# Query, key and value projections by one Strassen step in seven of eight images

## The chip, the cores and the metric

The kernel runs on one core of a Trainium2 chip. The metric is device time in microseconds (us) for one execution on the whole batch. TensorE (PE) multiplies matrices into PSUM; VectorE (DVE) and ScalarE (ACT) read PSUM and work on the on-chip memory SBUF; GpSimd (POOL) and SyncE (SP) mostly issue DMA transfers.

## What is computed

The batch has 8 images of 512 channels and 32 x 32 pixels, all in float32. Each image is group-normalised, goes through a block with two bottlenecks, and is added to its input. Cut to what matters:

```python
t = cbs(x, cv1_w, cv1_bn, 0)                    # 1x1 convolution, batch norm, silu
ys = [t[:, :C], t[:, C:]]                       # C = 256
for i in range(N):                              # N = 2 bottlenecks ("layers")
    yi = ys[-1]
    z = cbs(yi, m_cv1_w[i], m_cv1_bn[i], 1)     # 3x3 convolution
    z = bot_attention(z, m_qkv_w[i], m_rw[i], m_rh[i])
    z = silu(bn_eval(conv2d(z, m_cv2_w[i], 0), m_cv2_bn[i]))
    ys.append(yi + z)
return cbs(concatenate(ys, axis=1), cv2_w, cv2_bn, 0)

def bot_attention(x, qkv_w, rw, rh):            # 4 heads of 64
    q, k, v = conv2d(x, qkv_w, 0)               # 256 -> 3 x 256 channels, 1024 pixels
    logits = einsum('bhdi,bhdj->bhij', q, k + (rw + rh)) * 64 ** -0.5
    return einsum('bhij,bhdj->bhdi', softmax(logits), v)
```

So there are 16 projections to q, k and v: two layers in each of eight images. Each is a product of a 768 x 256 weight with a 256 x 1024 activation.

## The kernel before

Channels lie on the 128 partitions, so 256 channels are two blocks, called c, k or o in the code, and the 1024 pixels are two halves of 512. A loop over images, written out, runs per image: 3x3 convolution of layer 0 (`conv3x3`, matmuls at L756), projection (`project`), attention (`attention_fast`), 1x1 convolution `m2`, then the same for layer 1, then `cv2`. Parts of `cv1` of the next image, its group norm (`ahead` in layer 0), and parts of `cv2` are put behind attention groups by the dictionary `behind`. The convolutions use Winograd's scheme; `cv2` already uses a Strassen step (`strassen`) in all images but the last, with `product(..., onto=True)` accumulating a second product onto a PSUM tile that has been copied out in between.

`project` computes, for each c, kr (k plus the position terms rw and rh) and q: four matmuls of 512 columns each (two k blocks, two halves) into one PSUM tile (L321). ScalarE copies q out (L488); VectorE adds rw while it reads PSUM (L493), then rh (L494). v is computed transposed, with z as the stationary operand and 256 columns of weights moving (L505), and copied out by ScalarE (L510). In float32 each matmul appears in the trace as two records, each with its own weight load, so a projection has 32 records of 512 columns and 32 of 256.

`attention_fast` has four groups (c, half) of eight steps taken in pairs. A step computes logits into one PSUM tile (L540), ScalarE's exp writes them to a `pt` tile (L544), VectorE adds the pt tiles into `acc` for the softmax sums (L550, L552), and TensorE multiplies with v into `av` (L566), one pair behind the logits. At a group's end the sums go through a small matmul (L584), and `ao` is formed from `av` (L573, L574).

A tile framework orders the work: it gives each instruction a priority by its place in the program, plans each engine's order with a cost model when the program is built, and puts in the waits. `tc.issue_after` only adds an order on one engine. Tiles with the same tag share buffers: `big` in PSUM has three[...], `av` in PSUM one, `pt` three, and weights go through a ring `u` of five:

```python
def ring(shape, name):
    return const.tile(shape, F32, tag="u", name=name, bufs=5)
```

SP's DMA queue carries the loads into that ring, x, and the small transfers of the softmax sums; POOL's queue carries the residuals, the stores of the result and of prepared weights.

Of the kernel before, what the change touches and what calls it, by code (L numbers as in the profile page):

```python
# [52 lines left out]
P = 128  # L53
# [8 lines left out]
def kernel(  # L62
# [143 lines left out]
    def load_bottleneck(n):  # L206
        nc.sync.dma_start(qkv_sb[:, n], m_qkv_w[n].rearrange("(k p) o -> p k o", p=P))
        nc.sync.dma_start(rw_sb[:, n], m_rw[n].rearrange("(k p) f -> p k f", p=P))
        nc.sync.dma_start(rh_sb[:, n], m_rh[n].rearrange("(k p) f -> p k f", p=P))
        nc.sync.dma_start(m2_sb[:, n], m_cv2_w[n].rearrange("(k p) o -> p k o", p=P))  # L210

# [70 lines left out]
    def load_u(n, oc, i):  # L284
        u = new_u("u")
        nc.sync.dma_start(u, u_dram[n][oc][i])
        return u
# [7 lines left out]
    def img(ap):  # L295
        return ap.rearrange("p (h w) -> p h w", w=F)
# [4 lines left out]
    def stages(act, small, ps_big, ps_av, n_pt):  # L301
# [172 lines left out]
        def project(n, z):  # L474

            q = act.tile([P, NM, HW], F32, tag="q", name="q")
            kr = act.tile([P, NM, HW], F32, tag="k", name="kr")
            vT = act.tile([P, NJ, C], F32, tag="v", name="vT")

            def qk(c):  # L480
                for which in (1, 0):
                    o = which * C + c * P
                    ps = conv1x1(
                        lambda k: qkv_sb[:, n, k, o : o + P], lambda k, half: z[:, k, ts(half, HALF)], NM
                    )
                    for half in range(NH):
                        if which == 0:
                            nc.scalar.copy(q[:, c, ts(half, HALF)], ps[:, half, :])  # L488
                            continue
                        dst = img(kr[:, c, ts(half, HALF)])  # L490
                        rw = rw_sb[:, n, c, :].unsqueeze(1).to_broadcast([P, ROWS, F])
                        rh = rh_sb[:, n, c, ts(half, ROWS)].unsqueeze(2).to_broadcast([P, ROWS, F])
                        nc.vector.tensor_tensor(dst, img(ps[:, half, :]), rw, ALU.add)  # L493
                        nc.vector.tensor_tensor(dst, dst, rh, ALU.add)  # L494

            qk(0)
            per = NH * HALF // C
            for j0 in range(0, NJ, per):
                ps = ps_big.tile([P, per, C], F32, tag="big", name="v_ps")

                in_bank = per // NH
                for j in range(in_bank):
                    for k in range(NM):
                        for at in range(j, per, in_bank):
                            nc.tensor.matmul(  # L505
                                ps[:, at, :], z[:, k, ts(j0 + at, P)], qkv_sb[:, n, k, 2 * C : 3 * C],
                                start=(k == 0), stop=(k == NM - 1),
                            )
                for g in range(0, per, per // NH):
                    nc.scalar.copy(vT[:, j0 + g : j0 + g + per // NH, :], ps[:, g : g + per // NH, :])  # L510
            for c in range(1, NM):
                qk(c)
            return q, kr, vT

        def attention_fast(n, z, at, behind):

            q, kr, vT = project(n, z)
            behind.get(-1, lambda: None)()  # L520

            ao = act.tile([P, NM, HW], F32, tag="z", name="ao")
# [483 lines left out]
    for b in range(B):  # L1006
        more = b + 1 < B
        y1, y1n, y2 = ypad[b % 2], ypad[(b + 1) % 2], ypad[N]

        def u_of(n):  # L1010
            def of(oc):
                if b == 0 and oc == 1:
                    if n == 0:
                        with tc.issue_after(last.ins):
                            for i in range(PAIRS):
                                make(n, oc, [i])
                    else:
                        for k in range(NM):
                            raws[n, oc, k] = load_raw(n, oc, k, "kv"[k])
                        with tc.issue_after(last.ins):  # L1020
                            make(n, oc, [1])
                return [us.pop((oc, i)) if (oc, i) in us else load_u(n, oc, i) for i in range(PAIRS)]

            return of


        z = s.conv3x3(0, vs, u_of(0))
        if b == 0:
            load_bottleneck(1)
            raws[1, 0, 0] = load_raw(1, 0, 0, "y0", 2)  # L1030
            raws[1, 0, 1] = load_raw(1, 0, 1, "pt", 3)
        if more:
            xs = [load_x(act, b + 1, c, NX) for c in range(NX)]


        parts = {}


        norm = s.group_norm(xs) if more else iter(())
        groups = iter(range(NM * NH))  # L1040

        def ahead():
            nonlocal w1
            g = next(groups)
            next(norm, None)
            if g == 0:
                w1 = load_w1() if more else load_w2(1)
                if b > 0:
                    for at in ((0, 0), (0, 1), (0, 2), (1, 0)):
                        us[at] = load_u(1, *at)  # L1050
            if b == 0:
                if g == 0:
                    raws[1, 1, 0], raws[1, 1, 1] = load_raws_y0(1, 1)
                    make(1, 1, [2])
                    del us[1, 2]
                elif g <= NM:
                    make(1, 1, [0], [g - 1])

        def first():
            nonlocal nxt  # L1060
            if more:
                nxt = new_y0()
                s.cv1(w1, xs, nxt, y1n, Y1S[: NM // 2])
            else:
                parts[1] = s.cv2_part(w1, (y0, y1), 1)

        def second():
            if more:
                s.cv1(w1, xs, nxt, y1n, Y1S[NM // 2 :])
            else:  # L1070
                parts[2] = s.cv2_part(w1, (y0, y1), 2)

        NG = NM * NH
        behind = {g: ahead for g in range(NG)} | {NG: first, NG + 1: second}
        if b == 0:
            behind[-1] = lambda: make(1, 0, range(PAIRS))
        ao, check = s.attention_fast(0, z, b * N * NM * NH, behind)
        last = s.m2(0, ao, y1, lambda oc, half: inner(y2, oc, half))
        if more:
            s.cv1(w1, xs, nxt, y1n, Y0S)  # L1080
        else:
            parts[3] = s.cv2_part(w1, (y0, y1), 3)
            parts[0] = s.cv2_part(w1, (y0, y1), 0, range(NM))


        vs = s.tiles_in(y2)
        with tc.issue_after(last.ins):
            check()
        z = s.conv3x3(1, vs, u_of(1))
        w2 = ws = three = stored = None  # L1090
        begun = {}
        if b == 0:
            w2 = load_w2()

        def prepare():
            nonlocal stored, ws
            stored, ws = make_ws(w2)

        def ahead():
            nonlocal w2, three  # L1100
            if more:
                three = s.strassen(b, ws or load_ws(), y0, y1)
                for i in range(PAIRS):
                    us[0, i] = load_u(0, 0, i)
            else:
                w2 = load_w2()

        def first():
            if more:
                three[0]()  # L1110
            else:
                ks = range(NM, (1 + N) * NM)
                begun[0] = s.cv2_products(w2, (y0, y1, y2), 0, ks, ends=(ks[0], (2 + N) * NM - 1))

        def second():
            if more:
                three[1]()
            else:
                ks = range(2 * NM, (1 + N) * NM)
                begun[1] = ps_av.tile([P, NH, HALF], F32, tag="av", name="ps")  # L1120
                s.cv2_products(w2, (y0, y1, y2), 1, ks, begun[1], (ks[0], (2 + N) * NM - 1))

        behind = {1: ahead, NG: first, NG + 1: second}
        if b == 0:
            behind[0] = prepare
        ao, check = s.attention_fast(1, z, (b * N + 1) * NM * NH, behind)
        ylast = act.tile([P, NM, HW], F32, tag="v", name="ylast")
        last = s.m2(1, ao, y2, lambda oc, half: ylast[:, oc, ts(half, HALF)])
        with tc.issue_after(last.ins):
            check()  # L1130
        if more:
            three[2](y2, ylast, last, stored)
            with tc.issue_after(last.ins):
                vs = s.tiles_in(y1n)
        else:
            s.cv2(b, w2, (y0, y1, y2, ylast), begun, parts)
        y0 = nxt
# [94 lines left out]
```

## Time and profile before

| | |
|---|---|
| three timed runs | 2391.86 to 2392.54 us, median 2392.14 |
| span of the profiled execution | 2392.7 us |
| granted TensorE clock | 0.998 |
| L540 and L566, attention matmuls | 484.1 and 485.1 us, 4096 records each |
| L756, 3x3 convolutions | 307.9 us, 2720 records (and 40.8, 352) |
| L321 of the projections | 231.0 us, 512 records |
| L505, v of the projections | 115.8 us, 512 records |
| L544, exp | 494.9 us, 512 of 1023 ns |
| L552, softmax sums | 469.6 us, 384 of 1223 ns |
| L493 and L494, kr | 41.2 and 41.0 us, 64 of 686 and 682 ns |
| L488 and L510, copies of q and v | 34.4 us each, 64 of 589 ns |

A row is a group of instructions by line, engine and operation: busy time, count, mean duration. Matmuls are pipelined and their ends are modelled, so the mean duration of one is longer than the time until the next can start; starts in the timeline give the pitch. An engine's share of the span says little by itself; the waits say who waits for whom. A line such as `PE a L1 <- DVE b L2: 5.1, 5, 2.1` reads: TensorE, about to write a at line 1, waited for VectorE's b at line 2, 5.1 us in all, 5 times, the longest 2.1.

### The profile page before, as it was taken

To read this page: it belongs to the slowest core of one execution; us is meant where nothing else is said; L and a number is where in the kernel's file an instruction comes from. 1 tells how busy PE (TensorE), PEld (TensorE's weight loads), DVE (VectorE), ACT (ScalarE), POOL (GpSimd) and SP (SyncE) were. 2 spreads that over 40 slices of the span, in tenths; PEclk is the share of its full clock that TensorE was granted. 3 is DMA by queue.
4 is the path that set the end of the run, shared out by engine and by line. 5 is a ranking of instruction groups with operands and counts; after the bars stand their busy time and mean duration, and the time that the engine had idled before them with its cause. 6 is when DMAs were issued, how large, how long until landed. Compare 5 with 4: busy or idle time off the path is not lost.

```text
span 2392.7 us, 35333 instructions
## 1 busy us (share of the span) xinstructions
PE 2352.9 (98%) x14514; PEld 1176.4 (49%) x14514; DVE 1589.9 (66%) x2551; ACT 927.2 (39%) x1232; POOL 86.0 (4%) x301
## 2 busy tenths in 40 slices
PE   7999999999999999999999999999999999999998
PEld 4436355363553636446364453645536364463643
DVE  8866776666766667665586656766567765666654
ACT  1442524435244352433425344253432524326253
POOL 1000010000100001000010000100001000000001
PEclk9999999999999999999999999999999999999999
DMA  7412233030430305203161121601106020150202
GB/s 249 150 52 89 68 125 157 15 114 15 159 127 12 115 15 195 92 10 115 32 224 45 36 89 32 262 12 62 64 28 264 11 93 33 35 213 15 71 10 68
DMA packets 90728, 213.75 MB, mean 89 GB/s; under 512 B 27584, under 2 KB 49024, under 8 KB 77888
## 3 DMA queue, kind: packets, MB, share of 16 engines
q1 hardware_dynamic: 79360, 163.70, 20.0%
q0 software_dynamic: 11200, 47.72, 5.1%
q8 instruction: 116, 1.90, 0.3%
q14 instruction: 52, 0.43, 0.1%
HBM read 179.40 MB, written 31.98 MB: 88 GB/s over the span
## 4 chain that ended last, share of the span: by engine, by line
PE 93%; DVE 4%; DMA 1%; ACT 1%; issue 0%; SPq 0%; POOL 0%; DVEq 0%; ACTq 0%
PE ps L321 20%; PE av_ps L566 17%; PE l_ps L540 17%; PE c_ps L756 13%; PE c L811 8%; PE c_new L811 6%; PE m_ps L777 5%; PE v_ps L505 5%; DVE acc L552 1%; PE s_ps L584 1%; PE s_ps L602 1%; DMA rs<-r_dram 0%; DVE st L421 0%; DMA x<-in_x_dram 0%; DMA r_dram<-rc 0%
## 5 line engine op out<-in xcount | busy, mean ns | idle before, releaser
L544 ACT ACTIVATE pt<-l_ps 128x1024 f32<-128x1024 f32 x512 | 494.9, 1023 | 308.5 <-PE l_ps L540 307.0
L552 DVE TENSOR_TENSOR acc<-acc,pt 128x1024 f32<-128x1024 f32 x384 | 469.6, 1223 | 118.3 <-ACT pt L544 95.0
L566 PE MATMUL av_ps<-pt,vT 64*64 64x512 f32 x4096 | 485.1, 591 | 5.1 <-DVE ao L574 5.1
L540 PE MATMUL l_ps<-q,kr 64*64 64x512 f32 x4096 | 484.1, 590 | 0.0
L756 PEld LDWEIGHTS c_ps<-v_in,u 128*128 128x128 f32 x2720 | 306.7, 192 | 12.2 <-issue 9.7
L756 PE MATMUL c_ps<-v_in,u 128*128 128x128 f32 x2720 | 307.9, 275 | 4.6 <-DVE r_mid L388 1.7
L540 PEld LDWEIGHTS l_ps<-q,kr 64*64 64x64 f32 x4096 | 153.7, 133 | 278.6 <-issue 266.8
L566 PEld LDWEIGHTS av_ps<-pt,vT 64*64 64x64 f32 x4096 | 152.0, 133 | 281.5 <-issue 227.0
L321 PE MATMUL ps<-z,qkv_sb 128*128 128x512 f32 x512 | 231.0, 599 | 2.4 <-ACT z L306 2.1
L321 PE MATMUL ps<-x,w 128*128 128x512 f32 x512 | 227.5, 601 | 2.2 <-DVE x L455 2.2
L550 DVE TENSOR_TENSOR acc<-pt 128x1024 f32<-128x1024 f32 x64 | 78.4, 1225 | 134.0 <-ACT pt L544 134.0
L321 PEld LDWEIGHTS ps<-x,w 128*128 128x128 f32 x512 | 97.0, 192 | 130.6 <-issue 127.6
L493 DVE TENSOR_TENSOR kr<-ps,rw_sb 128x512 f32<-128x512 f32 x64 | 41.2, 686 | 178.1 <-PE ps L321 178.1
L321 PEld LDWEIGHTS ps<-z,qkv_sb 128*128 128x128 f32 x512 | 95.2, 191 | 110.4 <-issue 93.1
L811 PE MATMUL c_new<-t_in,ws 128*128 128x512 f32 x288 | 124.6, 592 | 0.0
L385 ACT COPY m<-c_ps 128x256 f32<-128x256 f32 x96 | 35.5, 370 | 227.7 <-PE c_ps L756 219.5
L505 PE MATMUL v_ps<-qkv_sb,z 128*128 128x256 f32 x512 | 115.8, 379 | 0.6 <-DVE r_ends L389 0.6
L777 PE MATMUL m_ps<-ao,m_sb 128*128 128x512 f32 x256 | 112.5, 592 | 0.0
L505 PEld LDWEIGHTS v_ps<-qkv_sb,z 128*128 128x128 f32 x512 | 97.2, 190 | 27.8 <-issue 16.2
L811 PEld LDWEIGHTS c_new<-t_in,ws 128*128 128x128 f32 x288 | 54.7, 190 | 68.9 <-issue 66.0
L306 ACT ACTIVATE m_kept<-m_kept,bh,sh 128x512 f32<-128x512 f32 x42 | 31.9, 806 | 146.0 <-DVE m_kept L895 86.3
L640 DVE TENSOR_TENSOR ao<-ao,rs 128x512 f32<-128x512 f32 x64 | 44.1, 688 | 63.4 <-DMA rs<-r_dram 62.8
(170 smaller groups left out, 2144.8 us busy)
## 6 DMA issues: line engine op xcount, KB each, us to landing
u<-u SPq DMA_DIRECT2D x85, 1024.0 KB
x<-in_x_dram SPq DMA_DIRECT2D x32, 512.0 KB
x_res<-in_x_dram POOLq DMA_DIRECT2D x28, 512.0 KB, 8.9
out_dram<-m_kept POOLq DMA_DIRECT2D x28, 512.0 KB, 7.5
w<-in_cv_w_dram SPq DMA_DIRECT2D x13, 1024.0 KB
u<-u_new POOLq DMA_DIRECT2D x12, 1024.0 KB, 5.8
rs<-r_dram SPq DMA_DIRECT2D x96, 128.0 KB
ws<-s SPq DMA_DIRECT2D x24, 512.0 KB
```

Source lines behind the costliest of these rows:

```text
L321: nc.tensor.matmul(ps[:, half, :], w_of(k), rhs_of(k, half), start=(k == begin), stop=(k == end))
L493: nc.vector.tensor_tensor(dst, img(ps[:, half, :]), rw, ALU.add)
L505: nc.tensor.matmul(ps[:, at, :], z[:, k, ts(j0 + at, P)], qkv_sb[:, n, k, 2 * C : 3 * C], start=(k == 0), stop=(k == NM - 1),)
L540: nc.tensor.matmul(ps[kh * HD : (kh + 1) * HD, hd, :], kr[r, c, o : o + HD], q[r, c, ts(half, HALF)], start=True, stop=True,)
L544: exp = nc.scalar.activation(pt[:, i], ps, AF.Exp, scale=SCALE)
L550: return nc.vector.tensor_tensor(accs[g], pt[:, 0], pt[:, 1], ALU.add)
L552: ins = nc.vector.tensor_tensor(accs[g], accs[g], pt[:, i], ALU.add)
L566: nc.tensor.matmul(avs[g][hd * HD : (hd + 1) * HD, kh, :], vT[r, j, o : o + HD], pt[r, i, hd, :], start=(j == 0), stop=(j == NJ - 1),)
L640: nc.vector.tensor_tensor(dst, dst, rs, ALU.mult)
L756: nc.tensor.matmul(ps[:, row, col, :], us[i][:, k, row, SLOT[col], :], vs[i][:, k, row, col, :], start=(k == 0), stop=(k == NM - 1),)
L777: nc.tensor.matmul(pss[oc][:, half, :], m2_sb[:, n, k, ts(oc, P)], ao[:, k, ts(half, HALF)], start=(k == 0), stop=(k == NM - 1),)
L811: nc.tensor.matmul(ps[:, o, :], w[:, k, ts(o, P)], rhs[part][:, c, :], start=(k == 0 and not onto), stop=(k == KB - 1), skip_group_check=onto,
```

## The change

A layer's weights are split in 2 x 2 blocks A (output block o, input block i; each block holds the 128 columns of q, k and v), z in 2 x 2 blocks B (channel block, pixel half). Four sums s1 to s4 of weight blocks are made once per layer, in the second attention of image 0, written to DRAM, and loaded into the ring with the convolution's second output block in images 1 to 7. Four sums t1 to t4 of z's blocks are made in each projection. Seven products replace eight; two pairs of them accumulate in PSUM (`onto=True`), with the first of each copied out (u, m5) in between. q, kr and v then come from sums on VectorE. Tiles t, u and m5 take the three `pt` buffers. Image 0 keeps `project`.

```diff
+    def make_sq(n):
+        (a11, a12), (a21, a22) = ([block_qkv(n, o, i) for i in range(2)] for o in range(2))
+        parts = [act.tile([P, 2, 3, P], F32, tag="x", name="sq_new", bufs=NX) for _ in range(2)]
...
+        nc.vector.tensor_tensor(s1, a21, a22, ALU.add)
+        nc.vector.tensor_tensor(s2, s1, a11, ALU.subtract)
+        nc.vector.tensor_tensor(s3, a11, a21, ALU.subtract)
+        nc.vector.tensor_tensor(s4, a12, s2, ALU.subtract)
+        for h, t in enumerate(parts):
+            nc.gpsimd.dma_start(sq_dram[n][:, 2 * h : 2 * h + 2], t)
+
+    def load_sq(n):
+        w = ring([P, 4, 3, P], "sq")
+        nc.sync.dma_start(w, sq_dram[n])
+        return w
...
+        def project_strassen(n, z, sq):
...
+            def product(ps, v, w, rhs, onto=False):
+                for o in range(2):
+                    nc.tensor.matmul(
+                        ps[:, o, :], w[:, o, :], rhs, start=not onto, stop=True, skip_group_check=onto
+                    )
+                for j in range(HALF // P):
+                    nc.tensor.matmul(
+                        v[:, ts(j, P)], rhs[:, ts(j, P)], w[:, 2, :], start=j == 0 and not onto, stop=True,
+                        skip_group_check=True,
+                    )
...
+            tt(t1, b12, b11, ALU.subtract)
+            ps_a, ps_b, ps_v = big(), big(), ps_av.tile([P, 2, HALF], F32, tag="av", name="pv_ps")
+            u, m5 = kept("u_z"), kept("m5_z")
+            product(ps_a, ps_v[:, 0], block_qkv(n, 0, 0), b11)
+            nc.scalar.copy(u[:, 0:2], ps_a)
+            nc.scalar.copy(u[:, 2], ps_v[:, 0])
+            product(ps_b, ps_v[:, 1], s1, t1)
+            nc.scalar.copy(m5[:, 0:2], ps_b)
+            nc.scalar.copy(m5[:, 2], ps_v[:, 1])
+            tt(t2, b22, t1, ALU.subtract)
+            tt(t3, b22, b12, ALU.subtract)
+            tt(t4, t2, b21, ALU.subtract)
+            product(ps_a, ps_v[:, 0], block_qkv(n, 0, 1), b21, onto=True)
+            q0, _, v0 = places(0, 0)
+            nc.scalar.copy(q0, ps_a[:, 0])
+            add_r(0, 0, ps_a[:, 1])
+            nc.scalar.copy(v0, v_of(ps_v[:, 0]))
+            product(ps_b, ps_v[:, 1], s4, b22, onto=True)
+            q1, k1, v1 = places(0, 1)
+            nc.scalar.copy(k1, ps_b[:, 1])
+            nc.scalar.copy(q1, ps_b[:, 0])
+            nc.scalar.copy(v1, v_of(ps_v[:, 1]))
+            ps_c, ps_w = big(), big()
+            product(ps_c, ps_w[:, 0], s2, t2)
+            tt(u[:, 0:2], ps_c, u[:, 0:2], ALU.add)
+            tt(u[:, 2], ps_w[:, 0], u[:, 2], ALU.add)
+            tt(k1, k1, u[:, 1], ALU.add)
+            add_r(0, 1)
+            tt(v1, v1, v_of(u[:, 2]), ALU.add)
+            tt(q1, q1, u[:, 0], ALU.add)
+            ps_d = big()
+            product(ps_d, ps_w[:, 1], s3, t3)
+            q2, k2, v2 = places(1, 0)
+            q3, k3, v3 = places(1, 1)
+            tt(k2, ps_d[:, 1], u[:, 1], ALU.add)
+            tt(q2, ps_d[:, 0], u[:, 0], ALU.add)
+            tt(v2, v_of(ps_w[:, 1]), v_of(u[:, 2]), ALU.add)
+            ps_e, ps_v = big(), ps_av.tile([P, 2, HALF], F32, tag="av", name="pv_ps")
+            product(ps_e, ps_v[:, 0], block_qkv(n, 1, 1), t4)
+            tt(k3, k2, m5[:, 1], ALU.add)
+            tt(q3, q2, m5[:, 0], ALU.add)
+            tt(v3, v2, v_of(m5[:, 2]), ALU.add)
+            tt(v2, v2, v_of(ps_v[:, 0]), ALU.subtract)
+            tt(k2, k2, ps_e[:, 1], ALU.subtract)
+            tt(q2, q2, ps_e[:, 0], ALU.subtract)
+            for half in range(NH):
+                add_r(1, half)
+            return q, kr, vT
...
-            q, kr, vT = project(n, z)
+            q, kr, vT = project(n, z) if sq is None else project_strassen(n, z, sq)
...
-                return [us.pop((oc, i)) if (oc, i) in us else load_u(n, oc, i) for i in range(PAIRS)]
+                got = [us.pop((oc, i)) if (oc, i) in us else load_u(n, oc, i) for i in range(PAIRS)]
+                if b > 0 and oc == 1:
+                    sq[n] = load_sq(n)
+                return got
...
-            behind[0] = prepare
+            behind |= {0: prepare, 2: lambda: make_sq(0), 3: lambda: make_sq(1)}
```

`add_r(c, half)` adds rw and then rh to kr in two operations; `places` names the parts of q, kr and v for an output block and a half.

## The prediction

> **What bounds the kernel now.** First I read the page: busy time of each engine, and the chain of work that ended last.
>
> ```profile
> PE 2352.9 (98%) x14514; PEld 1176.4 (49%) x14514; DVE 1589.9 (66%) x2551; ACT 927.2 (39%) x1232; POOL 86.0 (4%) x301
> ...
> PE 93%; DVE 4%; DMA 1%; ACT 1%; issue 0%; SPq 0%; POOL 0%; DVEq 0%; ACTq 0%
> ```
>
> TensorE is busy in all but 40 us, and the chain runs through it for 93%. Next the waits of TensorE, longest first:
>
> ```profile
> PE gm_ps L427 <- DVE mv L422: 11.6, 1, 11.6
> PE av_ps L566 <- DVE ao L574: 5.1, 5, 2.1
> PE ps L321 <- DVE x L455: 2.2, 1, 2.2
> PE ps L321 <- ACT z L306: 2.1, 2, 1.2
> ```
>
> The first is the start of the program; what is left is small. So a microsecond of matmul saved is a microsecond saved, provided that no new wait takes its place. Then the stage itself, a projection in a middle image, as the timeline of TensorE shows it (start, duration, records; consecutive groups overlap in their modelled ends, so I take differences of starts):
>
> ```profile
> 960.69 3.60 PE L321 MATMUL ps<-z,qkv_sb 128*128 128x512 f32 x8
> 964.13 1.03 PE L505 MATMUL v_ps<-qkv_sb,z 128*128 128x256 f32 x4
> 965.18 3.70 PE L321 MATMUL ps<-z,qkv_sb 128*128 128x512 f32 x8
> 968.72 6.21 PE L505 MATMUL v_ps<-qkv_sb,z 128*128 128x256 f32 x28
> 974.76 7.03 PE L321 MATMUL ps<-z,qkv_sb 128*128 128x512 f32 x16
> 981.72 3.66 PE L540 MATMUL l_ps<-q,kr 64*64 64x512 f32 x32
> 985.21 1.90 PE L566 MATMUL av_ps<-pt,vT 64*64 64x512 f32 x16
> ```
>
> From first projection matmul to first logit 981.72 - 960.69 = 21.03 us, with no gap; the second layer has 1118.08 - 1097.05, the same. VectorE in that stretch:
>
> ```profile
> 963.86 0.42 DVE L414 SCALAR_TENSOR_TENSOR z<-sd,r_ends 128x256 f32<-128x256 f32 x1
> 967.20 1.29 DVE L493 TENSOR_TENSOR kr<-ps,rw_sb 128x512 f32<-128x512 f32 x2 [2.92 <-PE ps L321]
> 968.41 1.28 DVE L494 TENSOR_TENSOR kr<-kr,rh_sb 128x512 f32<-128x512 f32 x2
> 978.39 1.29 DVE L493 TENSOR_TENSOR kr<-ps,rw_sb 128x512 f32<-128x512 f32 x2 [8.70 <-PE ps L321]
> 979.60 1.28 DVE L494 TENSOR_TENSOR kr<-kr,rh_sb 128x512 f32<-128x512 f32 x2
> 984.85 1.22 DVE L550 TENSOR_TENSOR acc<-pt 128x1024 f32<-128x1024 f32 x1 [3.96 <-ACT pt L544]
> 986.18 2.56 DVE L552 TENSOR_TENSOR acc<-acc,pt 128x1024 f32<-128x1024 f32 x2
> 988.65 1.87 DVE L421 BATCH_NORM_STATS2 st<-x 128x6 f32<-128x512 f32 x3
> ```
>
> It is mostly idle here. A 512-wide operation follows its neighbour after 0.605 us (968.41 - 967.20 for two). ScalarE:
>
> ```profile
> 964.32 1.52 ACT L306 ACTIVATE z<-z,bh,sh 128x512 f32<-128x512 f32 x2 [3.00 <-DVE z L414]
> 965.85 1.28 ACT L310 ACT_TABLE_LOAD   x1
> ```
>
> The second channel block of z ends at 965.84, 5.15 us after the convolution's last matmul was issued; today the k=0 matmuls and four v records fill that.
>
> **What the Trainium skill says.** "VectorE: DVE Perf Modes", section on the TRN2 errata, prices a float32 tensor_tensor at (N+151)/0.96 ns: 691 and 1224 ns for 512 and 1024; the trace has 686 (L493) and 1223 (L552). "TensorE: Matmul & The Clock Gate", section "Back-to-back issue gap", says that spacing is set by the matmul and its weight load together. The trace agrees: 192 convolution records of 128 columns took 21.44 us (1075.61 to 1097.05), 0.1117 each, against 0.1072 for a quarter of the 512-column pitch of 0.429. "ScalarE: Activation LUTs", section "What ACT_TABLE_LOAD costs", gives 1283 ns for a load; the trace shows 1283.
>
> **The change, part by part**, for the 14 projections of images 1 to 7.
>
> *TensorE.* Removed: 32 records of 512 columns and 32 of 256, 21.03 us. Added: seven products of 4 records of 512 and 8 of 128. 28 x 0.429 = 12.01; 56 x 0.1117 = 6.26; for 14 switches of shape 0.03 each, from the 0.1 and 0.04 us by which the 512-to-256 switches above exceed their pitch, 0.4. Sum 18.7. Gross gain 2.3 us a projection; bounds 2.0 (0.05 a switch, records of 0.115) and 2.75 (no switch cost).
>
> *VectorE.* 18 new operations, 17 of 512 and one of 1024: 17 x 0.605 + 1.13 = 11.4 us of pitch on top of the eight kr additions. *ScalarE:* eight copies of 0.589 become seven and two of 1.01, 1.4 us more, hidden in its gaps. What matters is order. Write T for the end of issue of the fifth product (s2, t2). TensorE then has two products, 2 x 2.67 = 5.3 us, and wants the first logit. VectorE has, from T - 0.7: u (1.13) and u of v, k1, two r additions, v1, q1, then k2, q2, v2 (done T + 6.05; q2 at T + 5.4), k3, q3, v3 (T + 7.85), the three subtractions (T + 9.65), four r additions (T + 12.1). The logits need PSUM: three big tiles, which the products hold. The first comes free with q2, some 0.2 us late; the next with v2; the third only at T + 9.65, so the third logit tile reuses the first after its exp. A tile takes 0.86 to fill (half of 1.72 for 16 records) and about 0.2 + 0.94 (3.77 / 4) to be drained, so four tiles on two buffers take about 4.0 us instead of the trace's 3.49: 0.2 + 0.5, and 0.1 for handing over. So 0.8, within 0.3 and 1.1.
>
> *The start of the projection.* The first two products need only z's first block and last 5.3 us, just over the 5.15. But the third and fourth accumulate onto PSUM that ScalarE must have copied, and the copies of m5 queue behind the silu and the table load: 965.84 + 1.5 + 1.01 + 0.59 = 968.9, where the fourth product wants them at 968.6 to 970. Bounds 0 and 1.35 (if the third product's v matmuls wait for m5's v copy, which lies in the same PSUM tile); I take 0.2.
>
> *After the projection.* VectorE is free for the softmax sums about 6.6 us after the first logit, not 3.1. Queued behind are the adds that free the three pt tiles, the first group's sums (before: last add 996.51, wanted 999.05) and the addition that frees the single av tile. In layer 1 gaps of 0.35, 0.88 and 1.79 us absorb it. In layer 0 four batch statistics of 0.6 us follow at once, slack is 2.5 us, and about 1 us can reach TensorE unless matmuls are reordered. Bounds 0 and 2; mean over layers 0.2.
>
> *DMA, ring, image 0.* A load of 768 KB joins SP's queue with the second half of the convolution's weights; its slot comes free a third of the way through the convolution, 14 us ahead of use, and a 1 MB transfer on the POOL queue lands in 5.8 us. Queued behind are x loads, w1 and later weights, wanted tens of us later, so nothing. Two stores on POOL lie beside attention. Eight 384-wide operations (0.55 us: 4.4 us) in image 0's second attention are fitted into VectorE's gaps of 0.8 to 1.8 us; 0 to 4, I take 1.
>
> *Sum.* 14 x (2.3 - 0.8 - 0.2 - 0.2) = 15.4; less 1 is 14.4. Against its own span, 2392.7 - 14.4 = 2378.3. The three timed runs have 2391.86 to 2392.54, so 2378.
>
> **The rivals.** *Nothing waits:* the order found fills every gap (as it does now around the silu) and the gross gain stays, 14 x 2.3 = 32 us, 2360. For: TensorE's waits are near zero today. Against: PSUM is full at the seam. *VectorE sets the seam (slower):* the place is from the fifth product to the end of the first attention group. It decides from 2.3 us of waiting a projection. If each of the 18 new operations costs 0.1 us more in semaphores or dependent issue (dependent neighbours show 0.72, not 0.605), the chain is 1.8 later: logits 0.8 + 1.2, layer 0's group end 1 + 1.9 averaged over two layers 1.45, sum 3.45 with none at the start; a loss of 1.15 x 14 = 16 us, 2408. For: VectorE at the seam has no slack on paper. Against: two thirds of it is idle elsewhere, and the adds can be interleaved. *Break-even:* ScalarE's m5 copies cost their full 1.35 and the seam 0.8, 2.15 against 2.3: 2390. *The change does not do what it says:* the products also need shape-switch time above 0.16 us, taking the whole gain; the trace's attention alternates shapes of weights every 16 records at 0.107 without loss, so unlikely.
>
> **How the numbers follow.** Forecast 0.44; nothing waits 0.26; break-even 0.12; slower seam 0.16; matmuls no faster 0.02. Break-even is shared between same and slower or faster: faster than 0.2% (4.8 us, about what a measurement of this kernel can tell from no change) 0.44 + 0.26 + 0.02 of it = 0.72; same 0.09; slower 0.19. The range reaches to 2359 for the full gain and to 2404 into the slower case; the forecast's own range is 2368 to 2386.
>
> **What would show it.** Right: 28 and 56 records a projection, 18.6 to 18.8 us of TensorE, first logit 18.9 to 19.6 us after the first product, a wait of the logits for VectorE (q2 or v2) of a few tenths, VectorE busy near 1770 us. Wrong: TensorE waiting over 1 us for m5's copy or for the av tile; 128-column records at 0.13 or more; VectorE's chain ending later than 13 us after the fifth product; weight loads of a product waiting for the sq load.

## The result, and the profile after

The changed kernel took 2383.66 us (median of 6 runs, 2381.73 to 2385.39), the kernel before 2391.92 beside it: ratio 0.9966, with a 95% interval from 0.9954 to 0.9979. That is 8.3 us, or 0.34%, where 14 us were forecast. The profiled execution has a span of 2383.3 us, 9.4 under before's 2392.7.

The page of the changed kernel, busy time of the engines and the chain:

```profile
PE 2326.4 (98%) x14794; PEld 1168.9 (49%) x14794; DVE 1751.7 (73%) x2811; ACT 947.7 (40%) x1246; POOL 88.1 (4%) x305
...
PE 81%; DVE 13%; DMA 4%; issue 2%; ACT 1%; SPq 0%; POOL 0%; DVEq 0%; ACTq 0%
```

TensorE has 26.5 us less to do, VectorE 162 more. VectorE's part in the chain rises from 4 to 13%, that of DMA from 1 to 4%: more of the program now ends behind them. TensorE's longest waits (the wait at the program's start, 10.8 us, is left out) name the place:

```profile
PE l_ps L656 <- DVE q L626: 12.2, 14, 0.9
...
PE av_ps L682 <- DVE ao L690: 6.5, 11, 2.1
PE l_ps L656 <- ACT pt L660: 4.0, 14, 0.3
PE c_ps L872 <- DMA u<-u: 2.8, 4, 1.5
```

Three waits are new. The two of the logits (`l_ps`) come 14 times each, once a projection; the one for loads into the ring comes in four convolutions and is taken up at the end. The timeline of TensorE at the same projection as before shows the first two in square brackets. Its lines are the first product's q and k, the v matmuls of the sixth, the last product, the four logit tiles and the first av matmul:

```profile
956.92 1.88 PE L556 MATMUL p_ps<-z,qkv_sb 128*128 128x512 f32 x4
...
971.77 1.05 PE L560 MATMUL p_ps<-sq,t_z 128*128 128x128 f32 x8
972.66 1.88 PE L556 MATMUL p_ps<-t_z,qkv_sb 128*128 128x512 f32 x4
974.38 1.05 PE L560 MATMUL pv_ps<-qkv_sb,t_z 128*128 128x128 f32 x8
975.45 1.95 PE L656 MATMUL l_ps<-q,kr 64*64 64x512 f32 x16
977.68 1.09 PE L656 MATMUL l_ps<-q,kr 64*64 64x512 f32 x8 [0.29 <-ACT pt L660]
979.64 1.09 PE L656 MATMUL l_ps<-q,kr 64*64 64x512 f32 x8 [0.87 <-DVE q L626]
980.55 1.90 PE L682 MATMUL av_ps<-pt,vT 64*64 64x512 f32 x16
```

From first product to first logit is 975.45 - 956.92 = 18.53 us, where it was 21.03: 2.5 won. From first logit to first av matmul is 5.10, where it was 3.49: 1.61 lost. The brackets count idle time after the modelled end of a matmul, so differences of starts are the better measure. VectorE in that stretch: the read that drains the fifth product (takes it out of PSUM), two reads of the sixth, the last read of the seventh, and the first softmax sum:

```profile
969.36 1.23 DVE L606 TENSOR_TENSOR u_z<-p_ps,u_z 128x1024 f32<-128x1024 f32 x1 [2.46 <-PE p_ps L556]
...
974.71 0.68 DVE L617 TENSOR_TENSOR q<-p_ps,u_z 128x512 f32<-128x512 f32 x1
975.31 0.68 DVE L618 TENSOR_TENSOR vT<-p_ps,u_z 128x512 f32<-128x512 f32 x1
...
978.90 0.68 DVE L626 TENSOR_TENSOR q<-q,p_ps 128x512 f32<-128x512 f32 x1
...
981.91 1.22 DVE L666 TENSOR_TENSOR acc<-pt 128x1024 f32<-128x1024 f32 x1
```

L626 ends at 979.58, and the fourth logit tile starts 0.06 later: it takes the buffer of the seventh product. In the table, made of differences of starts in one traced execution of each kernel, "projection" is first product to first logit, "seam" first logit to first av matmul, and "rest" first av matmul to the start of `m2`, in layer 0 and in layer 1. The value is that of most images, or about the median where they scatter. The times in us are medians of several runs, the ratios are to the kernel before on the same chip.

| kernel | projection | seam | rest, layer 0 / 1 | us | ratio (95%) |
|---|---|---|---|---|---|
| before | 21.03 | 3.49 | 69.8 / 68.85 | 2391.92 | |
| after | 18.52 | 5.10 | 70.2 / 68.85 | 2383.66 | 0.9966 (0.9954 to 0.9979) |
| no_sums | 18.44 | 3.49 | 69.8 / 68.85 | 2358.87 | 0.9859 (0.9844 to 0.9874) |
| three_before | 19.80 | 5.10 | 70.2 / 68.85 | 2400.91 | 1.0040 (1.0025 to 1.0056) |
| three_after | 19.80 | 5.10 | 70.2 / 68.86 | 2401.73 | 1.0043 (1.0028 to 1.0059) |
| chain_before | 19.73 | 4.34 | 71.56 / 68.85 | 2398.18 | 1.0028 (1.0017 to 1.0038) |
| chain_after | 18.52 | 5.10 | 71.53 / 68.85 | 2391.51 | 1.0004 (0.9995 to 1.0012) |
| drain7 | 18.52 | 3.60 | 71.71 / 68.9 | 2371.72 | 0.9923 (0.9910 to 0.9937) |
| drain7_pool4 | 18.52 | 3.60 | 72.2 / 68.9 | 2376.50 | 0.9938 (0.9925 to 0.9952) |
| drain7_pool8 | 18.52 | 3.48 | 71.13 / 69.48 | 2371.34 | 0.9914 (0.9899 to 0.9930) |
| drain7_r_later | 18.52 | 3.60 | 71.5 / 68.9 | 2374.59 | 0.9927 (0.9913 to 0.9940) |
| drain7_stats | 18.52 | 3.60 | 74.8 / 68.9 | 2390.95 | 0.9997 (0.9989 to 1.0006) |
| before_stats | 21.03 | 3.49 | 74.76 / 68.86 | 2418.28 | 1.0105 (1.0090 to 1.0121) |
| drain7_r_early | 18.45 | 3.48 | 69.8 / 68.85 | 2358.36 | 0.9862 (0.9846 to 0.9879) |

### The profile page after: what moved, and what is told of

Same layout as the page of the kernel before. It is cut to its first block, busy times and chain, and to the rows that moved or that the text cites. A ratio compares the mean times of both kernels' runs of the same rounds, so it can differ in the third digit from the quotient of the medians.

```text
span 2383.3 us, 36285 instructions
## 1 busy us (share of the span) xinstructions
PE 2326.4 (98%) x14794; PEld 1168.9 (49%) x14794; DVE 1751.7 (73%) x2811; ACT 947.7 (40%) x1246; POOL 88.1 (4%) x305
## 4 chain that ended last, share of the span: by engine, by line
PE 81%; DVE 13%; DMA 4%; issue 2%; ACT 1%; SPq 0%; POOL 0%; DVEq 0%; ACTq 0%
PE av_ps L682 16%; PE l_ps L656 14%; PE ps L344 12%; PE c_ps L872 11%; PE c L927 8%; PE c_new L927 6%; PE p_ps L556 5%; PE m_ps L893 5%; DVE acc L668 3%; PE pv_ps L560 2%; DMA u<-u 2%; DVE st L444 1%; PE s_ps L700 1%; DVE acc L666 1%; DVE u_z L606 1%
## 5 line engine op out<-in xcount | busy, mean ns | idle before, releaser
L656 PE MATMUL l_ps<-q,kr 64*64 64x512 f32 x4096 | 491.2, 593 | 16.3 <-DVE q L626 12.2
L927 PEld LDWEIGHTS c_new<-t_in,ws 128*128 128x128 f32 x288 | 54.7, 190 | 68.9 <-issue 66.0
L329 ACT ACTIVATE t<-m_ps,bh,sh 128x512 f32<-128x512 f32 x64 | 48.1, 776 | 83.9 <-PE m_ps L893 82.5
L556 PE MATMUL p_ps<-t_z,sq 128*128 128x512 f32 x168 | 81.3, 593 | 0.0
L373 POOL MEMSET w_rows<- 128x16 f32 x96 | 12.3, 128 | 1831.9 <-PE s_ps L700 1137.8
L893 PEld LDWEIGHTS m_ps<-ao,m_sb 128*128 128x128 f32 x256 | 48.6, 190 | 61.2 <-issue 61.2
L329 ACT ACTIVATE z<-z,bh,sh 128x512 f32<-128x512 f32 x64 | 48.6, 806 | 50.9 <-DVE z L437 50.8
```

The costliest lines, as they stand in the source:

```text
L329: return nc.scalar.activation(dst, src, AF.Silu, scale=sh[:, k : k + 1], bias=bh[:, k : k + 1])
L556: nc.tensor.matmul(ps[:, o, :], w[:, o, :], rhs, start=not onto, stop=True, skip_group_check=onto)
L656: nc.tensor.matmul(ps[kh * HD : (kh + 1) * HD, hd, :], kr[r, c, o : o + HD], q[r, c, ts(half, HALF)], start=True, stop=True,)
L893: nc.tensor.matmul(pss[oc][:, half, :], m2_sb[:, n, k, ts(oc, P)], ao[:, k, ts(half, HALF)], start=(k == 0), stop=(k == NM - 1),)
L927: nc.tensor.matmul(ps[:, o, :], w[:, k, ts(o, P)], rhs[part][:, c, :], start=(k == 0 and not onto), stop=(k == KB - 1), skip_group_check=onto,
```

## The experiments

The theory: the products save at least what was forecast, and VectorE's chain of sums gives most of it back, at first by holding PSUM. The rival: VectorE's backlog as such, the late softmax sums, costs the time. A second rival: something else in the change does, such as loads or copies.

**no_sums**: everything behind the fifth product on VectorE left out.

```diff
-            tt(u[:, 0:2], ps_c, u[:, 0:2], ALU.add)
...
-            tt(k2, ps_d[:, 1], u[:, 1], ALU.add)
...
+            nc.scalar.copy(k2, ps_d[:, 1])
+            nc.scalar.copy(q2, ps_d[:, 0])
+            nc.scalar.copy(v2, v_of(ps_w[:, 1]))
...
+            nc.scalar.copy(k3, ps_e[:, 1])
```

> All seven products stay, but the sums on VectorE behind the fifth product are left out: the fifth product is not read, and q, k and v of the second block are plain copies of products six and seven by ScalarE (so q, k and v are not the reference's). It bounds what the products alone bring. Theory: projection 18.5 us, seam 3.5 us, group ends as before: the kernel is 14 x (2.51 + 0.0) = 35 us under before, with the 2.5 us of other differences 2353 to 2358. Rival (something else in the change costs the time, such as the loads of the weight sums, the larger SP queue or the copies on ScalarE): 2365 or more.

It took 2358.87, 33 us under before, just above the 2353 to 2358 expected and clear of the second rival's 2365. Projection and seam are as expected; 14 x 2.59 = 36 us is their worth from the starts. So the seven products with their loads, copies and z's sums are worth about 33 us, and the sums behind them cost 25. The second rival falls.

**drain7**: ScalarE, idle at that time, copies the seventh product out.

```diff
+            e7 = act.tile([P, 2, HALF], F32, tag="acc", name="e_z", bufs=2)
+            nc.scalar.copy(e7, ps_e)
...
-            tt(k2, k2, ps_e[:, 1], ALU.subtract)
-            tt(q2, q2, ps_e[:, 0], ALU.subtract)
+            tt(k2, k2, e7[:, 1], ALU.subtract)
+            tt(q2, q2, e7[:, 0], ALU.subtract)
```

> The seventh product's PSUM tile is copied to SBUF by ScalarE, which is idle there, instead of being held until VectorE has subtracted it. Theory (PSUM tiles held by VectorE's chain set the seam): the third big tile comes free about 1 us after the last product instead of 4 us, the time from first logit to first av matmul falls from 5.10 to 3.5 to 3.8 us, and 14 x 1.3 to 1.6 = 18 to 22 us are won against the changed kernel: 2362 to 2366 us, ratio to before about 0.988 to 0.990. Rival (VectorE's backlog as such, the late softmax sums and the v sums behind them, sets the seam): VectorE has as much to do as before, so at most 0.3 us a projection, 2379 to 2384.

The seam fell to 3.60 as the theory has it; 14 x 1.5 = 21 us. But the kernel won only 12 and landed between the two forecasts. TensorE's timeline in a layer 0 projection (first logits, first av; then the sums of the first group and the next av tile) shows where the rest went, and one line of VectorE, the first softmax sum, shows why:

```profile
970.85 3.66 PE L658 MATMUL l_ps<-q,kr 64*64 64x512 f32 x32
974.45 1.95 PE L684 MATMUL av_ps<-pt,vT 64*64 64x512 f32 x16
...
989.12 0.64 PE L702 MATMUL s_ps<-acc,ones 128*32 128x256 f32 x8 [0.71 <-DVE acc L670]
990.77 1.95 PE L684 MATMUL av_ps<-pt,vT 64*64 64x512 f32 x16 [1.01 <-DVE ao L692]
```

```profile
977.32 1.22 DVE L668 TENSOR_TENSOR acc<-pt 128x1024 f32<-128x1024 f32 x1
```

The logits follow each other without a gap and TensorE arrives at the group's end earlier, but VectorE does not: its first sum starts 6.47 us after the first logit (977.32 - 970.85), as in the changed kernel (981.91 - 975.45 = 6.46). The rest of layer 0 grew by 9.3 us over seven images (from the starts), that of layer 1 by next to nothing. The waits lie in series: PSUM first, then, in layer 0, the backlog. Theory and rival are each half right.

**three_before, three_after**: three idle additions of 512, meant to stand ahead of the sixth product's reads, or behind the chain.

```diff
+            for _ in range(3):
+                tt(idle[:, 0], b11, b12, ALU.add)
```

> Three idle 512-wide additions (1.8 us of VectorE) stand in the chain ahead of the reads of the sixth product. They add work and change no result. Theory (PSUM tiles held by the chain): each projection's seam is longer by 1.2 to 1.8 us, 17 to 25 us in all, 2400 to 2409. Rival (backlog as such): the same time as with the three behind the chain.

> The same three idle additions stand behind the last of the chain, when no product's PSUM tile waits any more, but ahead of the softmax sums. Theory (PSUM tiles): the seam stays at 5.1 us; only layer 0, where the batch statistics follow, waits up to 1.8 us more for the av tile at the end of the first group: 0 to 12 us in all, 2384 to 2396. Rival (backlog as such): as much as three_before, 17 to 25 us.

Neither answers the question. The additions read only z's first block, and in both kernels they stand among the operations that finish z's second block. VectorE's timeline of three_before has the last of them there:

```profile
964.64 0.68 DVE L618 TENSOR_TENSOR idle<-z 128x512 f32<-128x512 f32 x1
```

and TensorE's has the third product waiting for z:

```profile
967.76 1.98 PE L556 MATMUL p_ps<-z,qkv_sb 128*128 128x512 f32 x4 [0.92 <-ACT z L329]
```

That three_before lands in the theory's range, and that both take the same time as the rival has it, therefore counts for neither. What they tell is another thing: 1.8 us of VectorE there cost 1.28 us of each projection (19.80 against 18.52).

**chain_before, chain_after**: the same three, now reading q1 or k3, which fixes their place.

```diff
+            for i in range(3):
+                tt(idle[:, 0], q1, q1 if i == 0 else idle[:, 0], ALU.add)
```

> Three idle 512-wide additions that read q1 stand on VectorE between q1 and the reads of the sixth product, so every later drain of PSUM is 1.8 us later. They add work and change no result. PSUM theory: the seam from first logit to first av matmul, or the wait ahead of the first logit, grows by 1.5 to 1.8 us in each of 14 projections, 21 to 25 us, and VectorE's backlog adds up to 1 us in layer 0 (7 us): 2404 to 2416. Backlog-only theory: the same time as with the three behind the chain.

> The same three idle additions, reading k3 after its r has been added: behind the last drain of PSUM, ahead of and between the first softmax sums. PSUM theory: seam as in the changed kernel (5.1 us); layer 0's first group end waits 1.5 to 1.8 us more, layer 1 (with slack of about 3 us) nothing: 7 x 1.5 to 1.8 = 10 to 13 us, 2394 to 2397. Backlog-only theory: as much as chain_before, 21 us or more.

Both lie below the theory's ranges, but the two kernels differ by 6.7 us, so where the work stands matters. chain_after kept the seam at 5.10, and layer 0's rest grew by 7.9 us over the seven images (from the starts); the time grew by as much, 7.9. chain_before moved the wait ahead of the first logit. Its longest waits of TensorE are these:

```profile
PE l_ps L659 <- DVE q L620: 17.0, 14, 1.2
PE av_ps L685 <- DVE ao L693: 10.5, 12, 2.0
```

L620 is the read of the sixth product's q. The projection is 1.21 longer and the seam 0.76 shorter: 14 x 0.45 = 6.3, less than the 21 expected. The seam is shorter when the logits start later, by which time more of the chain is done. With layer 0's 7.9, the same as in chain_after, it makes 14.2; measured 14.5.

**drain7_pool4, drain7_pool8**: drain7 with four or eight of the second channel block's operations on GpSimd.

```diff
-                add_r(1, half)
+                add_r(1, half, tt=nc.gpsimd.tensor_tensor)
```

> As drain7, and the four r additions of the second channel block, wanted only by the third attention group, go to GpSimd. VectorE is free for the softmax sums 2.4 us earlier. If drain7 left 1.5 us a projection in layer 0 to VectorE's backlog at the first group's end: it goes, 7 x 1.4 = 10 us, 2360 to 2364. If GpSimd's additions slow VectorE (shared access to SBUF) or the wait has another cause: no gain, 2370 or more.

> As drain7_pool4, and k3, q3 and the last subtractions of k2 and q2 go to GpSimd as well (eight operations in all). 2.4 us more are taken off VectorE, but m5's pt tile is freed later. Backlog theory: little is left to win after drain7_pool4, so the same within 3 us, 2358 to 2364, unless GpSimd is so slow (over 1.5 us an operation) that the third pt tile or the second channel block comes too late: then 2366 or more.

No gain: the intervals of both ratios overlap that of drain7. VectorE's softmax sums in drain7_pool4 while GpSimd runs:

```profile
976.68 2.07 DVE L668 TENSOR_TENSOR acc<-pt 128x1024 f32<-128x1024 f32 x1
978.85 4.10 DVE L670 TENSOR_TENSOR acc<-acc,pt 128x1024 f32<-128x1024 f32 x2
```

and GpSimd at that time:

```profile
973.42 2.79 POOL L577 TENSOR_TENSOR kr<-kr,rw_sb 128x512 f32<-128x512 f32 x1 [35.26 <-DVE kr L623]
976.29 1.38 POOL L578 TENSOR_TENSOR kr<-kr,rh_sb 128x512 f32<-128x512 f32 x1
```

An addition that takes 1.22 us elsewhere took 2.07 beside them. GpSimd took 2.4 us off VectorE, and three slower sums gave 2.4 back.

**drain7_r_later**: the four r additions behind the second group's first pair.

```diff
+                            if g == 1 and later:
+                                later[0]()
```

> As drain7, and the four r additions of the second channel block are placed behind the second attention group's first pair instead of at the end of the projection; they stay on VectorE. 2.4 us are taken off VectorE ahead of layer 0's first group end, and put into group 1, which also has four batch statistics. Backlog theory: the first group's waits of 1.7 us go, and up to 1 us comes back at the end of group 1: 7 x 0.7 to 1.7 = 5 to 12 us under drain7, 2360 to 2367. If not VectorE's order but its shared access or ScalarE makes the wait: no gain, 2370 to 2374.

The time is just above the range expected for no gain. The first group's waits went, and one of 1.88 came at the end of the second group:

```profile
1004.48 3.01 PE L687 MATMUL av_ps<-pt,vT 64*64 64x512 f32 x16 [1.88 <-DVE ao L695]
```

In layer 0 each of the first two groups has its own batch statistics, so work put off is work waited for later. The 16 records behind the wait took 3.01 us, where 16 take 1.90 elsewhere: the granted clock of TensorE was 0.59 from 1004.48 to 1008.60, and 1.00 before the wait.

**drain7_stats, before_stats**: the statistics one group later.

```diff
-            next(norm, None)
+            for _ in range(1 if b == 0 else (0, 1, 2, 1)[g]):
+                next(norm, None)
```

> As drain7, and in layer 0 of images 1 to 7 the batch statistics of the next image start one attention group later (none behind group 0, half behind group 1, the other half and the mean behind group 2). That takes 2.9 us off VectorE between the projection and the first group's end. Backlog theory: the waits for the sums and for the av tile at the end of layer 0's first group (0.71 + 1.01 us in drain7) go, and the 1 us by which layer 0's attention was longer than layer 1's before; 7 x 1.7 to 2.9 = 12 to 20 us under drain7, 2352 to 2360. If the wait only moves to the end of group 1 or 2, or to the mean: 2366 to 2374.

> A control: the kernel before, with the statistics one group later as in drain7_stats and nothing else. What it wins does not come from the projections. Layer 0's attention was 0.95 us longer than layer 1's (69.80 against 68.85) in six of seven images; if that was VectorE's statistics, 5 to 7 us go: 2384 to 2387. If the later mean makes TensorE wait: 2391 to 2396.

Both expectations failed. Against its own base the control lost more, 27 us; drain7_stats lost about 18 against drain7. In before_stats, the mean's matmul stands in TensorE's queue where VectorE has not got that far:

```profile
1026.97 0.56 PE L427 MATMUL gm_ps<-mv,gmat 128*128 128x4 f32 x2 [2.45 <-DVE mv L422]
1027.46 3.35 PE L540 MATMUL l_ps<-q,kr 64*64 64x512 f32 x16
1030.64 1.03 PE L566 MATMUL av_ps<-pt,vT 64*64 64x512 f32 x8
```

That is about half of the 5 us by which layer 0's rest grew. Of the other half, 1.5 us stand in the lines behind it: from start to start the 16 logit records take 3.18 us (1030.64 - 1027.46), where 16 take 1.72 elsewhere. The granted clock was 0.54 there, and 1.00 before and behind. The trace has such a stretch of 3.4 us at a granted clock of 0.5 in five of the six images with this wait.

**drain7_r_early**: drain7, with the r additions moved to where VectorE stands idle in the projection.

```diff
-            nc.scalar.copy(k1, ps_b[:, 1])
+            add_r(0, 1, ps_b[:, 1])
+            add_r(1, 1, m5[:, 1], m5[:, 1])
+            x = act.tile([P, HALF], F32, tag="h", name="r_z", bufs=2)
+            tt(img(x), rw_of(1), rh_of(1, 0), ALU.add)
...
-            add_r(0, 1)
...
-            for half in range(NH):
-                add_r(1, half)
+            tt(k2, k2, x, ALU.add)
```

> As drain7, with the position terms added where VectorE is idle in the projection: to k of the first block's second half straight from PSUM (in place of ScalarE's copy), to m5's k part as soon as it is copied (it reaches k3 with m5), and rw + rh of the remaining block summed ahead into a spare tile, so that five of the six r additions behind the fifth product leave VectorE's late chain, one stays: 3.0 us less between the fifth product and the softmax sums. Backlog theory: the waits of 0.71 and 1.01 us at the end of layer 0's first group go without a new one in group 1, because work moved into idle time and not behind: 7 x 1.7 = 12 us under drain7, 2358 to 2362. If VectorE's backlog only moved to group 1, as in drain7_r_later: 2370 to 2375.

It took 2358.36, ratio 0.9862 (0.9846 to 0.9879): 33.5 us under before, within the range expected, and as fast as no_sums with all its sums done. In the projection of the same image:

```profile
966.48 3.66 PE L663 MATMUL l_ps<-q,kr 64*64 64x512 f32 x32
969.96 1.90 PE L689 MATMUL av_ps<-pt,vT 64*64 64x512 f32 x16
...
983.80 0.64 PE L707 MATMUL s_ps<-acc,ones 128*32 128x256 f32 x8
984.37 1.95 PE L689 MATMUL av_ps<-pt,vT 64*64 64x512 f32 x16
```

No bracket is left at the seam or at the group's end. VectorE is busy for 1755.4 us in this kernel, 1751.7 in the changed one: the load is the same, and only the time at which it comes has moved.

## Why the prediction was right, and where it was off

**Direction and mechanism: right.** TensorE's saving was worth nearly all its time (33 of 36 us in no_sums), VectorE's chain behind the fifth product was the new wait, and PSUM was its place at the seam.

**Gross gain: too small.** 2.3 us a projection was forecast (2.36 by its own terms; its lower bound comes out at 1.9, not 2.0), 2.51 measured. The term for switches of shape was the error: I took 0.4 us for 14 switches. Eight records of 128 columns take 0.89 us from start to start (971.77 to 972.66), 0.111 each. 28 x 0.43 + 56 x 0.111 = 18.3, and no_sums has 18.44 in all: 0.2 is left for all switches. So the first logit came 18.5 us after the first product, ahead of the 18.9 to 19.6 forecast.

**The chain's times: right.** With T = 970.05, the start of the sixth product, u began at T - 0.69 (forecast T - 0.7), q2's last subtraction ended at T + 9.5 (9.65), and the sums started at T + 11.9 (12.1).

**The seam: forecast at half of what it was, and the main miss.** I forecast 0.8; it was 1.61. The step that failed is "four tiles on two buffers": that the third logit tile reuses the first after its exp, carried on to the fourth. The third did, and started 0.51 us late. The fourth was given the seventh product's buffer and waited for the end of the chain, 1.10 us, although the second's exp ends about a microsecond earlier. That this buffer was the place is shown by drain7, which empties it early and has a seam of 3.60; why the plan chose it is not. The wait was to be for q2 or v2 and a few tenths; it was for q2's last subtraction, 0.9 in each projection. This cost 14 x 0.8 = 11 us, set against 3 us of greater gross gain and 3 of no loss at the projection's start. That errors of opposite sign left the total within the forecast's own range is in part luck.

**Start of the projection: no wait** (0.2 forecast). ScalarE's second copy of m5 starts at 964.38, after silu and table load as worked out, but TensorE's order had put the third product's v matmuls (965.58) behind one matmul of the fifth product and one of the fourth. **Layer 0's first group end:** layer 0's rest grew by 3.5 us over seven images, 0.25 a projection against 0.2. Of these, 1.6 stand in image 2, whose rest is as long in no_sums, so not all of it is the backlog. **Image 0** lost nothing, where 1 us was forecast; up to the first changed projection the traced execution is 2.6 us ahead. Its unchanged second projection came out 1.7 us shorter (23.03 against 24.73): in the kernel before, TensorE's granted clock was 0.50 from 219.92 on for 3.41 us, in the changed kernel it was 1.00 throughout. no_sums, with the change in it, has 24.73 again, so this is no gain of the change. The next convolution was 1.4 shorter, as it also is in before_stats, which is without the change. Later convolutions lost 1.8. **Sum** of the starts: 14 x (2.51 - 1.61) - 3.5 + 2.6 - 1.8 = 9.9, against 9.6 to the last `m2`.

**Rivals.** "Nothing waits" gave 2360; that is what no_sums and drain7_r_early reach. "VectorE sets the seam" had the right place, but its premise failed: the new operations did not cost 0.1 us more each, the chain ended on time, and the seam gave back 1.61 of the 2.51 us, not all of it. GpSimd took no part in the result. DMA was forecast to cost nothing; the traced execution has 2.8 us of waits for loads into the ring, the kernel before none. Other kernels with the same loads have 0.2 to 1.6, and before_stats, without the new load, has 1.4, so it is not shown that the new load causes them.

## What to carry to other kernels

When matmuls are traded for sums, price the drain: list which PSUM tile each sum frees, and when the next stage needs that tile. An engine that stands idle at that time can empty the last one; here ScalarE did it for 1 us. Then look for the second wait behind the first: here removing one exposed nearly half of its worth at the next group's end. Moving sums into earlier idle time cured it here; putting them off or giving them to GpSimd did not.

## What the runs showed of the hardware

VectorE's large additions in SBUF were slower while GpSimd added too: in drain7_pool4 the 28 softmax sums of 1024 columns that ran wholly beside it took 2.06 to 2.12 us, those with nothing beside them about 1.22. Not every operation was slower: of the four 512-column operations of a projection that ran wholly beside it, three kept their 0.69. GpSimd's own 512-column additions took 1.4 to 2.9 us there, where VectorE's take 0.69; GpSimd was not measured alone.

Waiting cost TensorE more than the wait in some places: in before_stats a wait of 2.45 us was followed by 3.4 us at a granted clock of 0.5, which cost another 1.5 us. How long a wait must be for this was not measured.

Float32 matmul records of 128 columns, in groups of eight between groups of four of 512, kept their pace: 0.111 us each, and 18.44 us for a projection of 84 records.
